# One copy of the queries out of PSUM, and the gated channels turned one step ahead, in a hybrid recurrent, attention and sparse-FFN kernel

## The chip, the cores and the metric

The kernel runs on one core of a Trainium2 chip. The metric is device time in microseconds (us) of one execution; three executions are given and their median counts. TensorE (PE; its weight loads are the row PEld), VectorE (DVE), ScalarE (ACT), GpSimd (POOL) and SyncE (SP, which here only issues DMAs) each work through a queue of their own in order.

## The reference

The input `x` has 4 sequences of 1024 tokens with 256 channels. Four residual layers follow, each on the normalized `x`. The change touches the second and the third:

```python
x = x + lru(layernorm(x))
x = x + ffn(layernorm(x), ...)      # first call: "f1" in the kernel
x = x + attention(layernorm(x))     # 8 heads of 64, full softmax, keys from a latent of 64
x = x + ffn(layernorm(x), ...)      # second call, same weights: "f2"

# attention
q = (x @ Wq.T).reshape(b, t, 8, 64); k, v = up-projections of x @ Wkv_down.T
attn = softmax(q k^T / 8);  out = (attn v).reshape(b, t, 512) @ Wo.T

# ffn: two score vectors per token, each softmax cut to its 32 largest
out_branch = keep32(score_out) * (x @ weight)
in_branch  = (keep32(score_in) * x) @ weight
return out_branch + in_branch + bias
```

`keep32(s)` stands for the softmax with all but its 32 largest values set to zero; the reference writes it with `top_k` and a scatter.

## The kernel before

The work is tiled by 128 tokens: 32 tiles, 8 in a sequence. Stage one (to about 376 us of the profiled execution) holds the recurrent layer, the first eight FFN tiles and the preparation of the attention. Stage two (376 to about 1292 us) is the attention, with 24 FFN tiles of f1 and the heads of f2 interleaved. Stage three is f2's tiles.

Stage two is written as one main generator, `heads`, and a list `side` of generators. `heads` yields 256 times: 4 sequences x 2 halves (`nb`) x 4 pairs of heads (`g`) x 4 query tiles (`q`) x 2 heads (`j`). One such yield is called a step here. Every step makes 128x1024 scores in PSUM (L886, tile `sc`), their negated row maximum (L890, L892, tile `nm`), the exponentials (L894, tile `pr`), and then their transpose: for even `q` ACT and POOL split them into two float16 parts (L897, L898, tile `pd`) and a DMA on SP's queue transposes (L899, tile `d`); for odd `q` PE transposes (L905) and ACT copies (L910, tile `p`). `values_sum` multiplies with the values later (L930, tile `pmo`) and scales (L938, L940, L941).

`merge` takes one step of `heads`, then every side generator whose due time has come; each yield of a side generator moves its due time on by the number, or the next number of the list, given with it. That fixes program order. The order in each engine's queue is then made by the framework's scheduler, which simulates the program with costs of its own, takes program order as priority, and hands out buffers as they come free.

All side work and `pmo` share one PSUM tag, `"s"`, with two buffers: query products `pmq`, FFN logits `pl`, turned channels `px`, FFN products `pf`, output products `pmy`, `pt`, `pc`, `pml`, `pv`. A third tile waits until one of two is released by its last reader.

`queries` is called 32 times, 7 steps before its result is first used. It makes 128x512 query values for a pair of heads in `pmq` (6 matmuls) and needs them in `qs` in two forms: for head j, partitions of that head hold the value rounded to float32r, and the other 64 partitions hold the rest, value minus rounded value. `products` (L170) works in such two-part sums, and `split` (L160, L161) makes the two parts elsewhere, on ACT and DVE.

A fine FFN tile (`tile(..., fine=True)`, 24 of them) yields after its logits and exponentials, three times inside the search for the 32 largest (L674), after the search (L628 to L630), after the out branch (L636; `full` comes from DRAM), and at its end. The in branch scales `x` (L656, L657), gates it (L658, tile `xg`), turns it by two transposes (L682, `px`), splits it (`vt0`, `vt1`), and multiplies (L685 bias, L170 products, `pf`); L662 adds to `x`. With the list `[1, 1, 1, 1, 1, 2, 1]` the in branch runs two steps after the out branch.

Of the kernel before, what the change touches and what calls it, by code (L numbers as in the profile page):

```python
# [10 lines left out]
F32 = mybir.dt.float32  # L11
I32 = mybir.dt.int32
F32R = mybir.dt.float32r
# [3 lines left out]
ALU = mybir.AluOpType  # L17
# [4 lines left out]
P = 128  # L22
# [3 lines left out]
KD = D // P  # L26
# [131 lines left out]
def split(nc, hi, lo, src):  # L158

    last = nc.scalar.copy(hi, src).ins  # L160
    nc.vector.tensor_tensor(lo, src, hi.bitcast(F32), ALU.subtract)  # L161
    return last
# [17 lines left out]
class Banks:  # L180
# [5 lines left out]
    def tile(self, shape, tag, name):  # L186
        return self.pool.tile(shape, F32, tag=tag, name=name, bufs=self.bufs[tag])
# [300 lines left out]
class Ffn:  # L488
# [100 lines left out]
    def tile(self, i, sp, psum, tags, out=None, fast=False, parts=None, tt=None, fine=False):  # L589


        nc, w = self.nc, self.w
        pool = nc.vector if fast else nc.gpsimd
        x = self.x[i]
        blk, tk = i // 4, slice((i % 4) * P, (i % 4 + 1) * P)
        full = None
        if blk in self.full:
            full = sp.tile([P, D], F32, tag="full", name="full")
            nc.sync.dma_start(full, self.full[blk][:, i % 4, :])
        pl = psum.tile([P, 2, D], tags[0], "pl")  # L600
# [12 lines left out]
        nc.gpsimd.tensor_scalar(nm, m8[:, :, 0, 0], -1.0, 0.0, ALU.mult, ALU.add)  # L613
        for s in range(2):
            nc.scalar.activation(  # L615
                ex[:, s, :], pl[:, s, :], AF.Exp, bias=nm[:, s : s + 1], accum_out=ssum[:, s : s + 1]
            )
            self.last_exp = nc.scalar.activation(e8[:, s, :], m8[:, s, 0, :], AF.Exp, bias=nm[:, s : s + 1]).ins
        yield
        for r in range(nr):  # L620
            for s in range(2 if r else 0):
                self.ordered(nc.vector.max, m8[:, s, r, :], wk[:, s, :])
            for s in range(2):
                v, k = (wk, m8[:, s, r, :]) if r else (ex, e8[:, s, :])
                self.ordered(nc.vector.match_replace, wk[:, s, :], k, v[:, s, :], 0.0)
            if fine and r < nr - 1:
                yield
        pool.tensor_tensor(ex, ex, wk, ALU.subtract)  # L628
        rs = sp.tile([P, 2], F32, tag="rs", name="rs")
        nc.vector.reciprocal(rs, ssum)  # L630
        yield

        q = i % 4
        norm = self.norm[blk]
        if full is not None:
            nc.vector.scalar_tensor_tensor(full, full, rs[:, 0:1], ex[:, 0, :], ALU.mult, ALU.mult)  # L636
            ob = full
        else:
            if tt is not None:
                pf = psum.tile([P, D], tags[2], "pf")  # L640
                self.full_product(pf, tt, q)
            else:
                xn = sp.tile([P, D], F32, tag="fxn", name="fxn")
                with self.tc.issue_after(self.convolved):
                    nc.scalar.activation(
                        xn, x, AF.Identity, bias=norm[:, 1, q : q + 1], scale=norm[:, 0, q : q + 1]
                    )
                pf = self.product(sp, psum, tags, xn, None, parts)
            ob = sp.tile([P, D], F32, tag="ob", name="ob")
            nc.scalar.mul(ob, pf, rs[:, 0:1])  # L650
            pool.tensor_tensor(ob, ob, ex[:, 0, :], ALU.mult)  # L651
        yield

        xg = sp.tile([P, D], F32, tag="xg", name="xg", bufs=2)
        sc = sp.tile([P, 2], F32, tag="sc", name="sc")
        pool.tensor_scalar(sc, norm[:, :, q], rs[:, 1:2], 0.0, ALU.mult, ALU.add)  # L656
        nc.scalar.activation(xg, x, AF.Identity, bias=sc[:, 1:2], scale=sc[:, 0:1])  # L657
        pool.tensor_tensor(xg, xg, ex[:, 1, :], ALU.mult)  # L658
        nc.gpsimd.tensor_tensor(x, x, ob, ALU.add)
        pi = self.product(sp, psum, tags, xg, w.bias, parts)  # L660
        if out is None or fast:
            nc.vector.tensor_tensor(x, x, pi, ALU.add)  # L662
        else:
            yi = sp.tile([P, D], F32, tag="yi", name="yi")
            nc.scalar.copy(yi, pi)
            nc.gpsimd.tensor_tensor(x, x, yi, ALU.add)
        if out is not None:
            nc.sync.dma_start(out[i // 4][:, i % 4, :], x)
        yield
# [4 lines left out]
            ins = make(*args).ins  # L674
        self.last_topk = ins if self.keep else None

    def product(self, sp, psum, tags, v, bias, parts):

        nc, w = self.nc, self.w
        px = psum.tile([P, KD, P], tags[1], "px")  # L680
        for k in range(KD):
            nc.tensor.transpose(px[:, k, :], v[:, k * P : (k + 1) * P], w.ident)  # L682
        dst = psum.tile([P, D], tags[2], "pf")
        if bias is not None:
            nc.tensor.matmul(dst, w.ones, bias, start=True, stop=False)  # L685
        if parts:
            vt = [sp.tile([P, KD, P], F32R, tag=f"vt{i}", name=f"vt{i}", bufs=1) for i in range(2)]
            split(nc, *vt, px)
            products(
                nc,  # L690
                dst,
                [([t[:, k, :] for t in vt], [t[:, k, :] for t in parts]) for k in range(KD)],
                start=bias is None,
            )
            return dst
        vt = sp.tile([P, KD, P], F32, tag="vt", name="vt", bufs=2)
        nc.scalar.copy(vt, px)  # L697
        for k in range(KD):
            nc.tensor.matmul(  # L699
                dst, vt[:, k, :], w.wf[:, k, :], start=(k == 0 and bias is None), stop=(k == KD - 1)  # L700
            )
        return dst
# [70 lines left out]
class Attention:  # L773
# [68 lines left out]
    def queries(self, b, nb, g, psum, tag):  # L842

        nc, xnt = self.nc, self.xnt[b, nb]
        qs = self.qs[b, nb, g] = self.wp.tile([P, 2, 512], F32R, tag="qs", name="qs", bufs=2)
        pm = psum.tile([P, 512], tag, "pmq")
        products(
            nc, pm, [([t[:, k, g * P : (g + 1) * P] for t in self.wqk], [t[:, k, :] for t in xnt]) for k in range(KD)]
        )
        for j in range(2):  # L850
            mine, other = slice(j * HD, (j + 1) * HD), slice((1 - j) * HD, (2 - j) * HD)
            nc.scalar.copy(qs[mine, j, :], pm[mine, :])
            nc.vector.tensor_tensor(qs[other, j, :], pm[mine, :], qs[mine, j, :].bitcast(F32), ALU.subtract)  # L853
        yield

    def heads(self, b, psum):
# [183 lines left out]
def tile_kernel(ctx: ExitStack, tc: tile.TileContext, x_in, w_lru, vecs_in, rows, w_ffn, lin_t, w_attn, w_down, out):  # L1040
    nc = tc.nc
# [20 lines left out]
    w = Weights()  # L1062
# [8 lines left out]
    f1 = Ffn("f1", tc, bp, x, w)  # L1071
# [3 lines left out]
    with ExitStack() as c1:  # L1075
        psum = Banks(c1.enter_context(tc.tile_pool(name="ps1", space=PSUM)), {"pu": 2, "po": 2, "py": 2, "pt": 2})
# [38 lines left out]
        k = NBLK - 1  # L1115
# [14 lines left out]
    with ExitStack() as c2:  # L1130
        sp = c2.enter_context(tc.tile_pool(name="at_s", bufs=2))
# [3 lines left out]
        wfs = two([P, KD, D], "wf")  # L1135
# [48 lines left out]
        psum = Banks(c2.enter_context(tc.tile_pool(name="ps2", space=PSUM)), {"sc": 2, "t": 2, "s": 2})  # L1184
        at.hp = c2.enter_context(tc.tile_pool(name="at_h", bufs=1))
        fp = c2.enter_context(tc.tile_pool(name="f_s", bufs=2))
        side = []
# [22 lines left out]
        for i in range(TPB, NT):  # L1210
            n = i - TPB
            start = 1 + 6.75 * n if n < TPB else STEPS * (n // TPB) - STEPS + 48.25 + 8 * (n % TPB + 1)
            side.append((start, f1.tile(i, fp, psum, "sss", parts=wfs, fine=True), [1, 1, 1, 1, 1, 2, 1]))
        merge(chain(*(at.heads(b, psum) for b in range(B))), side)
        for j in range(2):
            last = at.output(B - 1, 1, psum, range(2 * j, 2 * j + 2), slice(PAIRS - 1, PAIRS), True)
# [1 line left out]
    with ExitStack() as c3:  # L1218
        psum = Banks(c3.enter_context(tc.tile_pool(name="ps3", space=PSUM)), {"pl": 2, "px": 3, "pf": 3})
        fp = c3.enter_context(tc.tile_pool(name="f_e", bufs=4))  # L1220
# [104 lines left out]
```

## Time and profile before

| | before |
|---|---|
| median of 3 executions | 1530.5 us (1527.78 to 1530.98) |
| profiled execution, own time | 1528.76 us |
| its span, first to last instruction | 1527.0 us |
| mean granted TensorE clock | 0.946 |
| busy over the span: PE / DVE / ACT / POOL | 84% / 78% / 67% / 45% |

The profile's rows name source line, engine, operation and tiles (`out<-in`), with a count, busy time and the mean duration of one. A row of waits says whose engine stood idle before which instruction, which instruction ended the idle time, then total us, number of times and the longest. A row of the timeline begins with the start and the duration in us; a bracket gives the idle time before the instruction and what ended it.

### The profile page before, as it was taken

The numbers are of one execution on the slowest core, as the hardware profiler recorded it, in microseconds if no ns is written. First come the engines' busy times: TensorE is split into PE (matmuls) and PEld (weight loads), VectorE is DVE, ScalarE is ACT, GpSimd is POOL, SyncE is SP. The second block draws the span as 40 slices with busy tenths as digits, with TensorE's granted clock in tenths as the row PEclk, the third lists the DMA queues.
The fourth block names the chain that finished last, engine by engine and source line by source line (L and its number), as shares of the span: only waits on it lengthen the run. The fifth ranks groups of instructions, "written<-read, shape, count | busy, mean of one in ns | idle before, by whom it ended". The sixth has DMA issues, their size and how long they took to land. (4 is left out here: it accounts for less than half of the span.)

```text
span 1527.0 us, 28727 instructions
## 1 busy us (share of the span) xinstructions
PE 1286.5 (84%) x10134; PEld 955.6 (63%) x10136; DVE 1184.6 (78%) x3682; ACT 1017.5 (67%) x2152; POOL 680.3 (45%) x849
## 2 busy tenths in 40 slices
PE   4879998697898898888998989889999999566675
PEld 3535465376677766766776767677777777334454
DVE  8976665697868887878768687777676675599998
ACT  5353433566887877797777787877777776475674
POOL 2033332161545454544544554454344444067776
PEclk9999999698999999999999999999999999688899
DMA  3110000321454343434433445334344545000000
GB/s 118 32 41 15 21 21 21 128 97 49 84 93 90 61 77 73 77 70 82 82 74 60 72 79 86 61 61 83 68 82 79 92 86 96 1 15 24 22 25 28
DMA packets 288609, 96.51 MB, mean 63 GB/s; under 512 B 268233, under 2 KB 284626, under 8 KB 288466
## 3 DMA queue, kind: packets, MB, share of 16 engines
q1 hardware_dynamic: 283024, 88.50, 28.7%
q10 hardware_dynamic: 5442, 6.18, 1.2%
q8 instruction: 80, 1.31, 0.4%
q14 instruction: 63, 0.52, 0.1%
HBM read 16.01 MB, written 11.53 MB: 18 GB/s over the span
## 5 line engine op out<-in xcount | busy, mean ns | idle before, releaser
L898 POOL TENSOR_TENSOR pd<-pr,pd 128x1024 f16<-128x1024 f32 x128 | 273.5, 2141 | 247.6 <-ACT pd L897 185.7
L890 DVE TENSOR_REDUCE nm<-sc 128x1 f32<-128x1024 f32 x256 | 308.5, 1217 | 78.9 <-PE sc L886 77.5
L894 ACT ACTIVATE pr<-sc,nm 128x1024 f32<-128x1024 f32 x256 | 285.9, 1119 | 84.6 <-DVE nm L892 47.0
L886 PE MATMUL sc<-kh,qs 128*128 128x512 f32 x512 | 184.3, 438 | 26.4 <-ACT pr L894 18.8
L886 PE MATMUL sc<-kl,qs 128*128 128x512 f32 x512 | 162.0, 397 | 0.0
L674 DVE MATCH_REPLACE8 wk<-m,wk 128x256 f32<-128x256 f32 x384 | 154.9, 406 | 0.1
L910 ACT COPY p<-ptp 128x512 f32<-128x512 f32 x224 | 124.1, 590 | 45.3 <-PE ptp L905 33.7
L674 DVE MAX8 m<-wk 128x8 f32<-128x256 f32 x384 | 151.3, 412 | 0.4
L930 PE MATMUL pmo<-p,la 128*64 128x128 f32 x2048 | 144.0, 289 | 6.1 <-ACT ft L524 2.9
L905 PE MATMUL ptp<-ident,pr 128*128 128x128 f32 x1024 | 138.3, 275 | 12.9 <-ACT pr L894 12.4
L930 PEld LDWEIGHTS pmo<-p,la 128*64 128x64 f32 x2048 | 122.8, 144 | 25.0 <-ACT ft L524 5.1
L905 PEld LDWEIGHTS ptp<-ident,pr 128*128 128x128 f32 x1024 | 115.6, 140 | 34.8 <-ACT pr L894 22.2
L897 ACT CAST pd<-pr 128x1024 f16<-128x1024 f32 x128 | 133.5, 1054 | 5.6 <-DMA d<-pd 4.6
L886 PEld LDWEIGHTS sc<-kh,qs 128*128 128x128 f32 x512 | 85.2, 195 | 51.1 <-ACT pr L894 29.8
L886 PEld LDWEIGHTS sc<-kl,qs 128*128 128x128 f32 x512 | 97.0, 190 | 23.2 <-issue 1.4
L930 PE MATMUL pmo<-d,lb 128*64 128x128 f16 x3072 | 103.4, 222 | 7.6 <-DVE qs L853 2.6
L930 PEld LDWEIGHTS <-lb 128*64 128x64 f16 x3072 | 92.2, 111 | 26.3 <-issue 20.1
L628 POOL TENSOR_TENSOR ex<-ex,wk 128x512 f32<-128x512 f32 x61 | 77.6, 1273 | 57.4 <-DVE wk L674 45.5
L926 POOL COPY rows<-rs 128x128 f32<-128x128 f32 x128 | 36.1, 294 | 124.4 <-PE pmo L938 76.3
L941 DVE TENSOR_TENSOR on<-pmo,rb 128x128 f32<-128x128 f32 x128 | 36.4, 285 | 66.8 <-ACT rb L940 66.3
L147 PE MATMUL pt<-ident,xn 128*128 128x128 f32 x256 | 47.8, 309 | 44.5 <-ACT xn L145 32.9
L699 PE MATMUL pf<-wf,vt 128*128 128x256 f32 x288 | 81.2, 427 | 4.6 <-ACT vt L697 4.2
(307 smaller groups left out, 2768.6 us busy)
## 6 DMA issues: line engine op xcount, KB each, us to landing
tt<-ft SPq DMA_DIRECT2D x16, 256.0 KB
tt<-tt SPq DMA_DIRECT2D x8, 512.0 KB
out<-x SPq DMA_DIRECT2D x32, 128.0 KB
x<-in_x ACTq DMA_DIRECT2D x6, 512.0 KB
pf<-pfs SPq DMA_DIRECT2D x12, 256.0 KB
full<-pf SPq DMA_DIRECT2D x24, 128.0 KB
d<-pd SPq DMA_TRANSPOSE x128
wa<-in_w_attn SPq DMA_DIRECT2D x2, 640.0 KB
```

Of the source, the lines that this page charges most:

```text
L147: nc.tensor.transpose(pt[:, k, i * P : (i + 1) * P], xn[:, k * P : (k + 1) * P], ident)
L628: pool.tensor_tensor(ex, ex, wk, ALU.subtract)
L674: ins = make(*args).ins
L699: nc.tensor.matmul(dst, vt[:, k, :], w.wf[:, k, :], start=(k == 0 and bias is None), stop=(k == KD - 1))
L886: nc.tensor.matmul(sc[:, sl], qs[:, j, q * P : (q + 1) * P], kk[:, sl], start=(i == 0), stop=(i == 1))
L890: nc.vector.tensor_reduce(nm, sc, AX.X, ALU.max, negate=True)
L894: nc.scalar.activation(pr, sc, AF.Exp, bias=nm, accum_out=ssum[:, j : j + 1])
L897: nc.scalar.copy(pd[:, 0, :], pr)
L898: nc.gpsimd.tensor_tensor(pd[:, 1, :], pr, pd[:, 0, :], ALU.subtract)
L905: nc.tensor.transpose(pt[:, kk, :], pr[:, kc * P : (kc + 1) * P], self.ident)
L910: nc.scalar.copy(dst, pt)
L930: nc.tensor.matmul(po[j * HD : (j + 1) * HD, 0, :], v, pts[j][:, c, :], start=(n == 0), stop=(n == len(terms) - 1),)
```

## The change

Part one, in `queries`: ACT copies the whole 128x512 product out of PSUM once, into a new float32 tile `q` in SBUF (one buffer). VectorE then copies each head's 64 partitions from `q` to `qs` in float32r, and POOL computes the rest from `q` and `qs`. Before, ACT made each rounded half from PSUM and VectorE each rest from PSUM.

Part two, in `tile` and `product`: a new function `turn` does the two transposes and the split. A fine tile calls it in the in branch's step, yields, and calls `product` with the finished `vt` in the next one. The list of due times changes from `[1, 1, 1, 1, 1, 2, 1]` to eight ones: scaling, gating, the addition of the out branch and turning come one step earlier than before, the product stays at its step. Other callers get `turn` inside `product` in the same order as before.

```diff
@@ tile
-        pi = self.product(sp, psum, tags, xg, w.bias, parts)
+        vt = None
+        if fine:
+            vt = self.turn(sp, psum, tags, xg)
+            yield
+        pi = self.product(sp, psum, tags, xg, w.bias, parts, vt)
@@ Ffn
+    def turn(self, sp, psum, tags, v, parts=True):
+        px = psum.tile([P, KD, P], tags[1], "px")
+        for k in range(KD):
+            self.nc.tensor.transpose(px[:, k, :], v[:, k * P : (k + 1) * P], self.w.ident)
+        if not parts:
+            return px
+        vt = [sp.tile([P, KD, P], F32R, tag=f"vt{i}", name=f"vt{i}", bufs=1) for i in range(2)]
+        split(self.nc, *vt, px)
+        return vt
+
+    def product(self, sp, psum, tags, v, bias, parts, vt=None):
+        nc, w = self.nc, self.w
+        if vt is None:
+            px = self.turn(sp, psum, tags, v, False)
         dst = psum.tile([P, D], tags[2], "pf")
         if bias is not None:
             nc.tensor.matmul(dst, w.ones, bias, start=True, stop=False)
         if parts:
-            vt = [sp.tile([P, KD, P], F32R, tag=f"vt{i}", name=f"vt{i}", bufs=1) for i in range(2)]
-            split(nc, *vt, px)
+            if vt is None:
+                vt = [sp.tile([P, KD, P], F32R, tag=f"vt{i}", name=f"vt{i}", bufs=1) for i in range(2)]
+                split(nc, *vt, px)
@@ queries
+        q = self.wp.tile([P, 512], F32, tag="q", name="q")
+        nc.scalar.copy(q, pm)
         for j in range(2):
             mine, other = slice(j * HD, (j + 1) * HD), slice((1 - j) * HD, (2 - j) * HD)
-            nc.scalar.copy(qs[mine, j, :], pm[mine, :])
-            nc.vector.tensor_tensor(qs[other, j, :], pm[mine, :], qs[mine, j, :].bitcast(F32), ALU.subtract)
+            nc.vector.tensor_copy(qs[mine, j, :], q[mine, :])
+            nc.gpsimd.tensor_tensor(qs[other, j, :], q[mine, :], qs[mine, j, :].bitcast(F32), ALU.subtract)
@@ tile_kernel
-            side.append((start, f1.tile(i, fp, psum, "sss", parts=wfs, fine=True), [1, 1, 1, 1, 1, 2, 1]))
+            side.append((start, f1.tile(i, fp, psum, "sss", parts=wfs, fine=True), [1, 1, 1, 1, 1, 1, 1, 1]))
```

More of the change, by code (lines that the diff above doesn't have):

```diff
@@ L675, in ordered @@
         self.last_topk = ins if self.keep else None
-    def product(self, sp, psum, tags, v, bias, parts):
-        nc, w = self.nc, self.w
+    def turn(self, sp, psum, tags, v, parts=True):
         px = psum.tile([P, KD, P], tags[1], "px")
         for k in range(KD):
-            nc.tensor.transpose(px[:, k, :], v[:, k * P : (k + 1) * P], w.ident)
+            self.nc.tensor.transpose(px[:, k, :], v[:, k * P : (k + 1) * P], self.w.ident)
[8 more added lines that the diff above has]
+            px = self.turn(sp, psum, tags, v, False)
         dst = psum.tile([P, D], tags[2], "pf")
```

## The prediction

> **What bounds the kernel now.** I first cut the span where the change lies, from the first score product to the last (busy time by window: PE, PEld, DVE, ACT, POOL; the counts in brackets).
>
> ```profile
> 376.00:1292.00 916.00, 822.39 (x8245) 655.14 (x8246) 687.13 (x1714) 700.90 (x1366) 428.76 (x420) 0.98 0.42 77
> ```
>
> PE works 822 of 916 us, 90%; ACT 77%, DVE 75%, POOL 47%. A step is 916/256 = 3.6 us. Nothing but PE can set this stage for long, so a gain must come out of PE's idle 93.6 us. Outside this stage no queue changes except for one query group at 365 us, which is used 8 us after it is done. Next I read what ended PE's idle time there.
>
> ```profile
> PE sc L886 <- ACT pr L894: 18.8, 22, 2.8
> PE ptp L905 <- ACT pr L894: 12.4, 16, 1.8
> PE pt L147 <- DVE qs L853: 9.0, 5, 2.1
> PE sc L886 <- DVE qs L853: 6.7, 7, 1.7
> PE pf L170 <- DVE nm L892: 5.1, 6, 1.3
> PE pmo L930 <- DVE qs L853: 4.4, 5, 1.6
> ...
> PE pf L170 <- ACT vt L160: 3.7, 9, 0.7
> ...
> PE pf L170 <- DVE vt L161: 3.0, 4, 1.5
> ...
> PE pmy L170 <- DVE qs L853: 2.6, 2, 1.3
> ```
>
> Four rows end with L853, the old query subtraction. Three of them (`pt`, `pmo`, `pmy`: 16.0 us) have no use for queries: they wait for a PSUM buffer of tag "s" that `pmq` holds. The fourth (`sc`, 6.7 us, 7 times) waits for the queries. Three rows (`pf`: 11.8 us) are the FFN product waiting for its split. The change aims at these 34.5 us. Then the timeline of one late query group, and rows on the port that POOL and DVE share:
>
> ```profile
> 804.29 1.62 PE L170 MATMUL pmq<-xnt,wqk 128*128 128x512 f32 x6
> 808.38 0.58 ACT L852 CAST qs<-pmq 64x512 fp32r<-64x512 f32 x1
> 810.49 2.14 POOL L898 TENSOR_TENSOR pd<-pr,pd 128x1024 f16<-128x1024 f32 x1 [2.50 <-ACT pd L897]
> 810.58 0.68 DVE L853 TENSOR_TENSOR qs<-pmq,qs 64x512 fp32r<-64x512 f32 x1
> 811.32 0.72 PE L886 MATMUL sc<-kh,qs 128*128 128x512 f32 x2 [1.66 <-DVE qs L853]
> 811.81 0.58 ACT L852 CAST qs<-pmq 64x512 fp32r<-64x512 f32 x1
> 813.99 0.69 DVE L853 TENSOR_TENSOR qs<-pmq,qs 64x512 fp32r<-64x512 f32 x1
> ```
>
> ```profile
> L636 DVE SCALAR_TENSOR_TENSOR full<-full,rs,ex x24: 474/864/2319, 402.1 to 1063.7; 128x256 f32<-128x256 f32 x24
> L853 DVE TENSOR_TENSOR qs<-pmq,qs x64: 683/689/694, 367.3 to 1255.3; 64x512 fp32r<-64x512 f32 x64
> L953 POOL TENSOR_TENSOR onp<-on,onp 128x512 fp32r<-128x512 f32 x28 | 35.9, 1280 | 20.3 <-ACT onp L952 16.3 <-DVE m L674 3.1 <-PE ptp L905 0.9
> L269 DVE TENSOR_SCALAR t<-st,cs_s 128x256 f32<-128x256 f32 x1 | 0.3, 339 | 0.0
> L269 DVE TENSOR_SCALAR t<-st,cs_s 128x128 f32<-128x128 f32 x1 | 0.3, 272 | 0.0
> ```
>
> In the timeline the PSUM buffer is held from 804.29 to 814.68, 10.4 us, because four instructions of two queues read it in turn, each late in its queue. Read off the same way, the 32 groups hold it 7.8 us on average, and 3.0 us up to the end of ACT's first copy.
>
> **The change part by part.**
>
> *Part one, PSUM.* ACT's single copy has the shape of L910's (590 ns). The buffer is free at its end: 3.0 us instead of 7.8. Of the 16.0 us of buffer waits I take away three quarters, **-12 us**; the rest stays because the copy itself can be late, as above (pmq done at 805.91, copy at 808.38). If the freed buffer is at once taken by other late work, it is worth nothing.
>
> *Part one, ACT.* 64 copies of 580 ns go, 37.1 us; 32 of 590 come, 18.9. ACT loses 18.2 of its 701 us. PE waits 31.2 us for `pr`; in proportion that is 0.8: **-1 us**.
>
> *Part one, POOL.* 64 subtractions of 64x512 come. The nearest row is L953, same output type and 512 elements, 1280 ns: +82 us, POOL to 56%. Half the partitions may make it no cheaper; less than 0.7 us (L658's 256 elements) or more than twice L953 has no row behind it. They write other partitions than they read, which no POOL row of before does. POOL itself is covered by its idle 487 us. Queued behind them are L898 and L926. Each subtraction first waits for VectorE's copy, so a `pd` can be late by that wait and 1.3 to 2.6 us, and its transposing DMA on SP with it; the rows of PE's waits have 1.9 us in all for these DMAs, so I cost it at 0, and at 32 x 1 us if the cover is gone.
>
> *Part one, VectorE.* 64 subtractions of 689 ns go: -44.1 us. 64 copies SBUF to SBUF come. No such copy is in the trace; L269 (one SBUF source) grows by 67 ns for 128 elements, so 512 cost 339 + 2 x 67 = 473 ns, 30.3 us. At the rate of a PSUM source it would be 690. Here a rule speaks against the change. L636 (two SBUF inputs) took 474 ns alone, up to 2319, 972 on average, while L853 with one PSUM input never left 683 to 694. The Trainium skill, "SBUF — State Buffer", "Who interferes with whom", says that VectorE and POOL share a port pair as an exclusive lock, that a VectorE copy in a two-port mode needs it, and that the loser waits for the whole instruction of the other. By the L853 row alone the new copies are free of it: -14 us of VectorE time. By the rule they wait like L636, 0.50 us each (which agrees with a 47% busy POOL and half of a 2.14 us `pd`): +32, so +18 net. A second copy right behind the first may find the port still its own, +16, so +2. I take the rule and the middle, +10, and +2 for L636-like rows under a fuller POOL (24 x 0.5 x 82/429). That is 1.7% of VectorE's time; a quarter of it on PE's path is **+3 us**.
>
> *Part one, lateness.* Now the first half is ready when one subtraction ends, 1.4 us after ACT's first copy (mean of 32). Afterwards: the same queue wait on VectorE (0.7), lock 0.5, copy 0.47, POOL's queue 0.3, subtraction 1.28: 3.2 us, **1.8 us later**; if a `pd` stands ahead in POOL's order, up to 5. In 25 groups the queries are ready 6 us or more before use, and it costs nothing. In the 7 rows above it is on PE's path: 7 x 1.8 = 13 us, up to 35. But those groups are late since their product had to wait for a buffer, which now comes earlier. I take half of 13: **+7 us**.
>
> *Part two.* POOL's `sc`, ACT's `xg`, POOL's gating and `x` addition, two transposes, ACT's and VectorE's split: all exist before and only come one step earlier; no DMA is issued in that step (`full` is loaded at the tile's start, on SP). POOL stands at L656 for VectorE's `rs` already (45.2 us of its waits), with `pd` behind it; one step earlier can lengthen that, at POOL's cost alone. What moves on PE: the product no longer waits for a split issued just before, 11.8 us. A step of 3.6 us covers ACT's 0.39 and VectorE's 0.41 with their queues. Against it, the transposes follow the gating more closely (0.4 us of waits now); I let 3 us remain: **-9 us**. If the scheduler puts product right behind turn again, 0. Bias product and `pf` no longer take the second PSUM buffer while `px` holds the first; the row for that is small and I count nothing.
>
> Sum: -12 - 1 + 3 + 7 - 9 = -12 us. A PE at 90% hands some of it back in new waits for `pr`; I take **-10**. On the profiled execution's own 1528.76 us (span 1527.0 plus 1.8 around it) that gives 1518.8. The median is 1.7 higher, so I forecast 1530.5 - 10 = **1520.5 us**.
>
> **The rivals.**
>
> *Late queries (slower).* The score product waits for POOL. For: POOL's order is strict, `pd` takes 2.14 us, the copy in front can be locked out as long, and the late groups are the rule in the second and third sequence (slack 0.1 us). Price: if the buffers do not bring their products forward and a `pd` lies ahead, 7 x 5 = +35, and part one's other terms -12 - 1 + 3; with part two at 0 to -9 the end is 1530.5 + 16 to + 25, 1547 to 1556; with a delay of 3.5 us (+25) and half the buffer gain, 1530.5 + 25 - 7 + 3 - 9 = 1543. It decides from about 3.5 us of delay on the seven groups (25 us), where it outweighs the 22 us of -12, -1 and -9 with the +3. Against: POOL is half idle and the other 25 groups have slack.
>
> *Stalls re-form (no change).* The buffer waits turn into waits for `pr`, as ACT and VectorE are at three quarters and the scores have two buffers only. For: the two largest rows are these. Then 1528 to 1533.
>
> *The order does not follow.* The engines' order comes from a simulated schedule. If product follows turn at once, and freed buffers go to lower-priority work, the edit does less than it says: -1 + 3 + 13 = +15, 1545.
>
> *More than forecast.* All 16.0 and 11.8 us go and the late groups (6.7) vanish, less 3: -31, 1499.
>
> **How the numbers follow.** As forecast, 1508 to 1527: 0.44. More than that: 0.06. Within 0.2% of 1530.5 (1527.4 to 1533.6; about what a measurement of this kernel can tell from no change): 0.12. Late queries: 0.28, order: 0.10. So faster 0.50, same 0.12, slower 0.38. Faster and slower both hold much; the likeliest case alone is 1508 to 1527. For 8 in 10 the range goes from 1504 to 1546, leaving about one in ten out at either end.
>
> **What would show it.** Right: the rows `pt`, `pmo`, `pmy` <- qs nearly gone, `pf` rows below 4 us in sum, VectorE's copies near 0.5 us with a maximum near 2.5 (lock), POOL's subtractions at 1.28 us. Wrong: `sc` <- POOL `qs` over 20 us, or PE's idle time in this stage still above 90 us with `pr` as releaser. A PE busy time that differs by more than 5 us would mean that something outside these waits moved.

## The result: slower by 0.4%, where faster by 10 us was forecast

| | before | after |
|---|---|---|
| median | 1527.93 us (22 executions) | 1534.76 us (22 executions) |
| ratio, 95% interval | | 1.004 [1.003, 1.005] |
| profiled execution, own time | 1528.76 us | 1535.12 us |
| its span | 1527.0 us | 1533.4 us |
| mean granted TensorE clock | 0.946 | 0.931 |
| PE busy over the span | 1286.5 us | 1300.0 us |

The change costs 6.8 us by the medians and 6.4 us by the two profiled executions. PE executes the same matmuls in both (10134 and 10136 of them are in the traces) and is busy 13.5 us longer. The profile after, busy time by window (columns: length, then PE, PEld, DVE, ACT, POOL with counts, granted clock, DMA share, GB/s), cut late in stage one, at the first score product and at the end of the last:

```profile
0.00:291.40 291.40, 239.22 (x884) 144.71 (x884) 217.17 (x791) 124.76 (x239) 79.14 (x159) 0.93 0.15 51
291.40:380.90 89.50, 72.71 (x320) 53.19 (x319) 74.14 (x304) 53.02 (x128) 37.95 (x54) 0.84 0.19 65
380.90:1298.90 918.00, 828.57 (x8248) 659.66 (x8249) 692.57 (x1715) 681.41 (x1336) 513.31 (x483) 0.97 0.43 77
1298.90:1533.40 234.50, 159.50 (x688) 105.78 (x686) 208.40 (x874) 136.39 (x418) 136.81 (x218) 0.82 0.06 20
```

The same view of before:

```profile
0.00:290.00 290.00, 237.09 (x884) 144.08 (x884) 216.73 (x791) 124.64 (x239) 78.29 (x157) 0.94 0.12 39
290.00:376.00 86.00, 69.83 (x319) 51.99 (x318) 71.87 (x304) 53.59 (x129) 36.03 (x54) 0.88 0.31 109
376.00:1292.40 916.40, 822.79 (x8248) 655.44 (x8249) 687.37 (x1714) 701.30 (x1367) 429.11 (x421) 0.98 0.42 77
1292.40:1527.00 234.60, 156.83 (x688) 104.10 (x686) 208.63 (x874) 137.99 (x418) 136.89 (x218) 0.85 0.07 21
```

Read length minus PE busy as PE's idle time. Stage one: 4.9 us longer, all of it busy time (306.9 to 311.9). Stage two: 1.6 us longer, made of 5.8 us more busy time and 4.2 us less idle time (93.6 to 89.4). Stage three: unchanged in length. So PE's idle time in stage two did shrink, by less than half of the forecast, and two things outweigh that gain: stage two starts late, and PE takes longer for the same matmuls while the granted clock is lower in every row.

What ended PE's idle time in stage two of after (who waits, what released it; total us, times, longest; the rows used below, the others are left out):

```profile
PE sc L903 <- ACT pr L911: 23.1, 25, 2.7
PE ptp L922 <- ACT pr L911: 16.2, 20, 1.9
PE pmq L170 <- DVE on L958: 9.1, 5, 2.2
PE pmo L947 <- DVE on L958: 4.6, 6, 2.0
PE pf L170 <- DVE nm L909: 3.7, 5, 1.1
PE pmo L947 <- ACT q L866: 2.8, 4, 0.9
PE pmo L947 <- DMA d<-pd: 2.7, 3, 1.8
PE pf L170 <- ACT vt L160: 2.2, 6, 0.4
PE sc L903 <- POOL qs L870: 2.2, 3, 0.9
PE pl L554 <- DVE on L958: 1.4, 1, 1.4
PE px L685 <- DVE on L958: 0.8, 2, 0.4
PE pf L170 <- DVE vt L161: 0.6, 1, 0.6
PE pmy L170 <- DVE on L958: 0.6, 1, 0.6
```

The rows of before that end with the scaling of the attention's result (`on`):

```profile
PE pmy L170 <- DVE on L941: 1.5, 1, 1.5
PE pt L147 <- DVE on L941: 1.3, 1, 1.3
PE pmo L930 <- DVE on L941: 0.6, 1, 0.6
PE pf L685 <- DVE on L941: 0.5, 2, 0.3
```

The three rows `pt`, `pmo`, `pmy` behind the query subtraction (16.0 us before) are gone; 2.8 us behind the new copy `q` are what is left of them. The score product's wait for queries fell from 6.7 us to 2.2. In their place stand waits for the same two PSUM buffers, now released by `on`: 16.5 us in five rows (9.1 + 4.6 + 1.4 + 0.8 + 0.6), where `on` ended 3.9 us before. The waits for `pr` grew from 31.2 to 39.3 us.

The queries themselves (minimum, median, maximum in ns), two rows of VectorE by shape (busy us and mean ns), and one slow copy in the timelines of POOL and VectorE (its row holds a pair of copies; the first ends at 471.09):

```profile
L869 DVE CAST qs<-q x64: 397/424/2255, 370.6 to 1258.2; 64x512 fp32r<-64x512 f32 x64
L870 POOL TENSOR_TENSOR qs<-q,qs x64: 1259/1295/1469, 371.8 to 1259.8; 64x512 fp32r<-64x512 f32 x64
```

```profile
L869 DVE CAST qs<-q 64x512 fp32r<-64x512 f32 x64 | 33.4, 522 | 9.1 <-ACT q L866 8.1
L636 DVE SCALAR_TENSOR_TENSOR full<-full,rs,ex 128x256 f32<-128x256 f32 x24 | 29.6, 1232 | 11.3 <-POOL ex L628 11.3
```

```profile
468.66 2.15 POOL L915 TENSOR_TENSOR pd<-pr,pd 128x1024 f16<-128x1024 f32 x1 [3.29 <-issue]
469.86 1.68 DVE L869 CAST qs<-q 64x512 fp32r<-64x512 f32 x2
```

POOL's subtraction costs what its nearest row said. Of VectorE's 64 copies, 58 took 397 to 426 ns. The other six took 1226 to 2255 ns; each began while a `pd` subtraction was running on POOL, and each ended about 0.28 us after that subtraction did.

**Where stage two loses its start.** Before 360 us the change itself adds no instruction to any queue, and yet the queues differ. SyncE's timeline, first of before, then of after:

```profile
263.14 28.28 SPq L527 DMA_DIRECT2D tt<-ft  x6
293.53 0.83 SPq L561 DMA_DIRECT2D tt<-tt  x2
294.41 1.50 SPq L712 DMA_DIRECT2D wa<-in_w_attn  x2
```

```profile
264.52 0.51 SPq L527 DMA_DIRECT2D tt<-ft  x1
267.28 0.82 SPq L561 DMA_DIRECT2D tt<-tt  x2
268.15 0.91 SPq L727 DMA_DIRECT2D wa<-in_w_attn  x2
...
280.86 11.88 SPq L527 DMA_DIRECT2D tt<-ft  x4
```

The attention's weights (`wa`) are loaded 26 us earlier, in front of four of the recurrent layer's transfers. PE's queue is ordered differently too, and this is what it does some 30 us ahead of the attention, first before, then after:

```profile
349.34 1.99 PE L567 MATMUL pfa<-wf,tt 128*128 128x256 f32 x8 [2.04 <-ACT ob L650]
352.78 1.13 PE L567 MATMUL pf<-wf,tt 128*128 128x256 f32 x4 [1.45 <-ACT pfs L581]
```

```profile
348.18 0.38 PE L685 MATMUL px<-ident,xg 128*128 128x128 f32 x2
354.36 2.07 PE L567 MATMUL pf<-wf,tt 128*128 128x256 f32 x4 [5.81 <-ACT pfs L581]
```

Before, the eight `pfa` products stand between two short waits. After, they come later and PE stands still for 5.81 us in one piece; then the four `pf` products take 2.07 us instead of 1.13. The trace's clock records explain the second number:

```
granted clock up to 384 us, from the last rise ahead of these products (start, length in us)
before   1.0 from 311.2, 58.0   0.5 from 369.2, 10.2
after    1.0 from 305.3, 47.8   0.5 from 353.0,  6.8   1.0 from 359.9, 13.7   0.5 from 373.5, 10.2
```

Over the span, PE ran at half clock for 164.5 us before and 211.6 us after (54.6 to 68.8 in stage one, 37.5 to 57.5 in stage two, 72.4 to 85.3 in stage three). What that does to one matmul is seen in stage two of after: the score product of `kh` takes 630 ns in the median for the 20 that lie wholly in a stretch of half clock, and 396 ns for the 490 outside.

### The profile page after: what moved, and what is told of

Same layout as the page of the kernel before. It is cut to its first block, busy times and chain, and to the rows that moved or that the text cites. A ratio compares the mean times of both kernels' runs of the same rounds, so it can differ in the third digit from the quotient of the medians.

```text
span 1533.4 us, 28814 instructions
## 1 busy us (share of the span) xinstructions
PE 1300.0 (85%) x10136; PEld 963.3 (63%) x10136; DVE 1192.3 (78%) x3682; ACT 995.6 (65%) x2120; POOL 767.2 (50%) x913
## 4 chain that ended last, share of the span: by engine, by line
PE 43%; DVE 33%; ACT 11%; issue 5%; POOL 4%; DMA 2%; ACTq 0%; POOLq 0%; DVEq 0%
PE sc L903 9%; PE pmo L947 8%; DVE wk L678 7%; DVE nm L907 6%; DVE m L678 5%; PE ptp L922 4%; ACT pr L911 3%; PE po L437 3%; PE pmy L170 2%; PE pu L170 2%; POOL qs L870 2%; PE pl L556 2%; PE pz L452 1%; PE pfa L567 1%; ACT pd L914 1%
## 5 line engine op out<-in xcount | busy, mean ns | idle before, releaser
L903 PE MATMUL sc<-kh,qs 128*128 128x512 f32 x512 | 189.3, 447 | 26.5 <-ACT pr L911 23.1
L922 PE MATMUL ptp<-ident,pr 128*128 128x128 f32 x1024 | 139.5, 278 | 16.5 <-ACT pr L911 16.2
L947 PE MATMUL pmo<-p,la 128*64 128x128 f32 x2048 | 138.9, 281 | 5.3 <-ACT ft L524 1.5
L947 PEld LDWEIGHTS pmo<-p,la 128*64 128x64 f32 x2048 | 117.0, 139 | 26.0 <-issue 5.3
L870 POOL TENSOR_TENSOR qs<-q,qs 64x512 fp32r<-64x512 f32 x64 | 86.5, 1352 | 67.9 <-DVE qs L869 65.2
L714 PE MATMUL pf<-wf,vt 128*128 128x256 f32 x288 | 85.3, 439 | 3.3 <-ACT vt L712 2.6
```

The lines of the kernel that those rows point to most:

```text
L714: nc.tensor.matmul(dst, vt[:, k, :], w.wf[:, k, :], start=(k == 0 and bias is None), stop=(k == KD - 1))
L870: nc.gpsimd.tensor_tensor(qs[other, j, :], q[mine, :], qs[mine, j, :].bitcast(F32), ALU.subtract)
L903: nc.tensor.matmul(sc[:, sl], qs[:, j, q * P : (q + 1) * P], kk[:, sl], start=(i == 0), stop=(i == 1))
L922: nc.tensor.transpose(pt[:, kk, :], pr[:, kc * P : (kc + 1) * P], self.ident)
L947: nc.tensor.matmul(po[j * HD : (j + 1) * HD, 0, :], v, pts[j][:, c, :], start=(n == 0), stop=(n == len(terms) - 1),)
```

## The experiments

All are compared with before, which was measured again beside each group of kernels (medians of 1527.9 to 1530.2 us); a ratio, with its 95% interval, is against that before. "Start" is the first score product in the profiled execution: 376.0 us before, 380.9 after. Where an engine's order of instructions is said to be that of another kernel, it was read from the two traces.

### Part two alone

```diff
 (the change, but queries as before: two copies by ACT, two subtractions by VectorE from PSUM)
```

> Part two alone: fine tiles turn and split one step ahead, queries as before. If part two does its own work and part one carries the loss, this is 5 to 9 us faster than before (1519 to 1523) with the waits of the FFN product (11.8 us) cut to 4 to 7. If the loss lies in part two, it is about as slow as the changed kernel (1533 to 1536). If any change of the program moves the time by what a new instruction order brings, it lands anywhere within 8 us of before, whatever its waits do.

Measured: 1540.22 us, 1.0071 [1.0055, 1.0086]. Part two alone is no gain but the larger loss. The profiled execution puts it into the first sequence of stage two, 231.4 us long against 220.3:

```profile
378.50:609.90 231.40, 203.50 (x1925) 160.43 (x1925) 185.50 (x473) 177.57 (x357) 112.39 (x116) 0.96 0.45 78
```

PE has 44 more matmuls there than before (1881), is busy 8.0 us longer and idle 3.1 us longer. The separate step has moved work into this sequence, and the next two give only 2.7 us back. The start is 2.5 us later than before although no engine's order differs from before ahead of 400 us, so a shift of this size is what single executions differ by.

### Part one alone

```diff
 (before, with the change's queries: one copy, q, VectorE copies, POOL subtracts)
```

> Part one alone: one copy out of PSUM, split by VectorE and POOL; FFN tiles as before. If VectorE and POOL locking each other out carries the loss (late row maxima), this is as slow as the changed kernel or slower (1534 to 1542), with VectorE's copies at 0.5 us and more and the exponentials' waits for nm above 85 us. If part one is sound, it is 3 to 8 us faster than before. If the order alone decides, it is anywhere within 8 us, and the stage before the attention is some 4 us longer than before, as in the changed kernel.

Measured: 1532.43 us, 1.0015 [1.0001, 1.0029]. Start at 380.8, as late as with the whole change; the second sequence is 8.6 us shorter than before. A late start and a gain in stage two stand side by side, so part one has to be taken apart.

### The buffer alone

```diff
+        if (b, nb, g) == (0, 0, 0):
+            q = self.wp.tile([P, 512], F32, tag="q", name="q")
+            nc.gpsimd.memset(q[:, 0:1], 0.0)
         for j in range(2):   # queries as before
```

> The kernel before with the new tile q reserved in SBUF but used by nothing (one element column is cleared once by POOL). No engine has other work. If the new buffer alone changes where tiles lie and with it the order of all queues, the first score product comes 2 to 5 us later as in the changed kernel and the time differs from before by 2 to 8 us. If the loss comes from the work that the change moves, this equals before within 0.2%.

Measured: 1533.74 us, 1.0028 [1.0019, 1.0038]. The place is reserved and hardly touched, and the kernel is slower by more than with part one whole. Windows and the same stop in PE's timeline of this kernel:

```profile
291.00:379.50 88.50, 72.69 (x319) 53.18 (x318) 73.00 (x303) 53.62 (x129) 35.47 (x53) 0.85 0.20 66
379.50:1299.90 920.40, 827.30 (x8248) 660.68 (x8249) 687.66 (x1714) 700.41 (x1367) 428.79 (x421) 0.97 0.43 77
```

```profile
353.84 2.07 PE L567 MATMUL pf<-wf,tt 128*128 128x256 f32 x4 [5.81 <-ACT pfs L581]
```

The same 5.81 us of standing still, the same 2.07 us, half clock from 352.7 for 6.8 us, `wa` loaded at 267.60. In stage two its idle time is that of before (93.1 us) and its busy time is 4.5 us more, with 48.2 us of half clock. So both halves of the loss, the late start and the slower matmuls, appear with the reserved place alone. The profiled execution is the slowest of its 14 (1537.38 us), so the size of the second half is overstated here.

The early order follows the full place without exception. Five kernels reserve it in this pool (after, and the experiments of this section, the one before and the next, and "Subtraction on VectorE"): all load `wa` at 267.6 to 269.5 us, all have the stop of 5.81 us, and they start at 379.5 to 381.5. The other twelve, before among them, load `wa` at 293.7 to 297.0, stop for at most 2.04 us there and start at 374.3 to 378.7. Up to the first query group at 370 us every engine's order in this kernel is that of after. By which path a place in SBUF changes the schedule no run shows.

### First query group in the old form

```diff
+        if tag == "at":  # the group made ahead of stage two
+            (old copies and subtractions)
+        else:
             (the change's)
```

> The changed kernel, but the one query group that is made before the attention stage is made in the old way. If the 4.9 us that the changed kernel loses before its first score product come from that group's longer chain (copy, copy, subtraction on three engines), the first score product returns to about 376 us and the total falls by 3 to 5 us. If they come from the buffer and the order, the first score product stays at 380 us and the total at 1533 to 1537.

Measured: 1534.37 us, 1.0025 [1.0011, 1.0039]. Start still at 381.5. The chain of copy, copy and subtraction of the first group is not what delays stage two.

### The buffer in a pool that is opened later

```diff
-        q = self.wp.tile([P, 512], F32, tag="q", name="q")
+        q = self.hp.tile([P, 512], F32, tag="q", name="q")   # part one alone, first group in the old form
```

> Part one alone, with the new tile q placed in the pool of the attention stage that is opened last, and the first query group made in the old way, so that nothing before the attention stage has reason to move. If the buffer in the early pool costs 3 to 5 us before the first score product, that product is back at 376 to 377 us and the time falls to 1524 to 1528, below before, with the granted clock near 0.944. If part one has no gain of its own, the time stays at 1530 to 1534.

Measured: 1534.73 us, 1.0029 [1.0018, 1.0040], start at 378.7. Ahead of the attention this gives the old order back (`wa` at 296.71 us, no stop of 5.81 us), and the start lies at the upper end of the kernels with that order. The expected gain did not come: stage two takes 921.7 us, against 912.9 in part one alone. With the new place in another pool the loss lies in stage two.

### Subtraction on VectorE

```diff
-            nc.gpsimd.tensor_tensor(qs[other, j, :], q[mine, :], qs[mine, j, :].bitcast(F32), ALU.subtract)
+            nc.vector.tensor_tensor(qs[other, j, :], q[mine, :], qs[mine, j, :].bitcast(F32), ALU.subtract)
```

(in part one alone)

> Part one alone, but the subtraction is VectorE's too, from q and qs in SBUF; POOL gets no new work. If POOL's 82 us of subtractions and the port that it shares with VectorE carry a loss in part one, this is 2 to 6 us faster than part one with POOL (1532.4), with the exponentials' waits for nm lower. If VectorE's own time matters more (64 subtractions of about 0.7 us and 64 copies), it is 2 to 6 us slower. If neither, it is within 2 us.

Measured: 1563.56 us, 1.0214 [1.0201, 1.0228], 31 us more than part one alone. The stage's window, and VectorE's subtraction by shape:

```profile
381.50:1328.90 947.40, 832.40 (x8248) 663.85 (x8249) 727.49 (x1776) 682.69 (x1336) 436.13 (x421) 0.97 0.42 75
```

```profile
L855 DVE TENSOR_TENSOR qs<-q,qs 64x512 fp32r<-64x512 f32 x64 | 56.3, 880 | 2.0
```

A loss of 2 to 6 us was the case nearest to this. VectorE is busy 727 us of 947, PE's idle time rises to 115 us, and the stage is 34.5 us longer than in part one alone (912.9 us). The exponentials wait for VectorE's row maxima 126.6 us, against 92.3 in part one alone: 34.3 us more. So a subtraction of 56.3 us on VectorE delays the row maxima, though it is busy only 77% of the stage; a share that the new order has in this was not separated. In part one alone POOL takes the same 64 subtractions, is busy 56% of the stage, and PE waits 1.7 us for them. Giving the subtraction to POOL is the sound part of the change.

### Turned at the old due times

```diff
-                [1, 1, 1, 1, 1, 1, 1, 1]
+                [1, 1, 1, 1, 1, 2, 0, 1]      # part two alone: a yield, but turn and product in one step
```

> Part two alone with the due times of before: scaling, gating and turning stay two steps after the out branch and the product follows in the same step; only the order of split and bias product differs in program order. If the loss of part two (10.9 us) comes from moving the gating and turning a step forward, this equals before within 3 us. If it comes from the new order that any change of these instructions brings, it is 4 to 12 us slower than before.

Measured: 1529.54 us, 1.0000 [0.9990, 1.0011]. Start 374.4, first sequence 220.9 us. Every engine executes its instructions in the order of before, from beginning to end, so this is before once more: the rewritten functions and the added yield change nothing, and the loss of part two alone comes with its due times. Whether asking for the gating earlier does it, or any new order would, this run cannot tell, as it made no new order.

### A buffer of half the size

```diff
-            q = self.wp.tile([P, 512], F32, tag="q", name="q")
+            q = self.wp.tile([P, 256], F32, tag="q", name="q")   # the reserved place again
```

> The kernel before with a reserved tile of half the size of q (256 columns), one column cleared once by POOL. The order before the attention stage stays as before almost to its end. If the loss of the reserved full tile (4.4 us) comes from the stage before the attention (first score product at 379.5 us), this has its first score product at 376 us and loses at most 2 us. If the attention stage's own new order counts, it differs from before by 2 to 6 us in either direction.

Measured: 1528.93 us, 0.9992 [0.9983, 1.0001]. Start 376.0.

```profile
290.00:376.00 86.00, 70.87 (x319) 52.62 (x319) 71.69 (x303) 53.35 (x129) 36.20 (x55) 0.88 0.32 109
376.00:1289.70 913.70, 818.50 (x8248) 651.58 (x8249) 687.12 (x1714) 701.59 (x1367) 429.43 (x421) 0.99 0.43 78
```

The extra instruction on POOL is the same as with the full buffer, and the loss is gone. It is the size of the reserved place that sets off the other order. But for that one column this kernel does the very work of before, and every engine does it in the order of before, from beginning to end. So the 4.3 us by which its PE busy time in stage two differs from before, with 26.8 us of half clock instead of 37.5, is what two executions of one order differ by.

### Part one without a new buffer

```diff
-        q = self.wp.tile([P, 512], F32, tag="q", name="q")
+        q = self.sp.tile([P, KD, 256], F32, tag="ft", name="q", bufs=1).rearrange("p a b -> p (a b)")
```

`q` shares the buffer of the FFN's tile `ft`.

> Part one alone without a new buffer: q takes the SBUF tile ft of the same size, which only the heads of f2 use 14 times. The order before the attention stage stays as before almost to its end. If part one gains 3 to 4 us inside the attention stage and loses 4 to 5 before it only through the buffer, this is 3 to 6 us faster than before (1524 to 1527) with the clock at 0.943 or more. If part one has no gain of its own, 1528 to 1534.

Measured: 1525.54 us, 0.9975 [0.9963, 0.9987]. Part one is a gain once nothing is reserved for it: 0.40% between this and part one alone.

### Product one step later

```diff
-                [1, 1, 1, 1, 1, 1, 1, 1]
+                [1, 1, 1, 1, 1, 2, 1, 1]      # part two alone: turn at the old step, product one later
```

In this kernel the last tile of a sequence is added after the next sequence's normalization has read it: that addition is left out of what the attention sees, and a wait with it.

> Part two alone, but scaling, gating and turning stay at the step of before and the product goes one step later. The split still lies one step ahead of its product, so the waits of the FFN product fall as with part two. If the loss of part two (10.9 us) comes from the gating chain being asked for a step earlier, this is within 3 us of before. If any spacing of the two steps gives it (a new order, less often a full clock), it is 4 to 12 us slower.

Measured: 1536.44 us, 1.0044 [1.0027, 1.0061]. This is the second case: another spacing of the two steps costs time too, without any earlier gating, though this kernel has the omission in it. Moving the product instead of the turning is no remedy.

### Both parts, no new buffer, at three due times

The old step for turn and product (`[1, 1, 1, 1, 1, 2, 0, 1]`):

> Part one without a new buffer, and part two with the due times of before (turning and product in one step). If the two losses found (the buffer and the earlier step) are all that stands against the change, this is the fastest kernel: 1523 to 1527. If every rewrite draws a new order whose idle stretches and clock scatter by a few us, it lies between 1525 and 1536 and the clock tells where.

Measured: 1527.47 us, 0.9981 [0.9970, 0.9992]. Every engine's order is that of part one without a new buffer (1525.54 us), so this says nothing of part two; the 1.9 us between the two medians, of 22 executions each, are what one order measured twice differs by.

The product one step later (`[1, 1, 1, 1, 1, 2, 1, 1]`, with the omission of the kernel above):

> Part one without a new buffer, and part two with the product one step later instead of the gating one step earlier. If only the earlier gating harms, 1522 to 1528. If the split ahead of its product harms in itself, it is slower than before by 3 to 10 us, as part two alone.

Measured: 1506.72 us, 0.9853 [0.9829, 0.9877]. It would be the fastest, but for what it leaves out. The same with the last tile of each sequence begun half a step earlier, so that nothing is left out:

```diff
+            start -= 0.5 if n % TPB == TPB - 1 else 0
```

> Part one without a new buffer; turning at its old step and the product one step later, with the last tile of each sequence half a step earlier so that its sum is read by the next sequence as in the reference. If the gain of e12 (22 us) came from the wait that it left out, this is back at 1522 to 1532. If it came from the later product, it is at 1505 to 1512.

Measured: 1526.54 us, 0.9979 [0.9969, 0.9989]. So the 22 us hung on the omission, and the later product is worth nothing by itself. That they are a wait at the sequences' boundaries is not shown: the same omission in part two alone brought nothing (1536.44 us with it, 1533.69 without, below).

### The whole change without its buffer

```diff
-        q = self.wp.tile([P, 512], F32, tag="q", name="q")
+        q = self.sp.tile([P, KD, 256], F32, tag="ft", name="q", bufs=1).rearrange("p a b -> p (a b)")
```

> The whole change, but q takes the tile ft and no new buffer is reserved. If the buffer is the larger part of the loss, this is at 1526 to 1530, at or below before. If part two with its earlier step is the larger part, it stays at 1533 to 1540.

Measured: 1523.94 us, 0.9962 [0.9948, 0.9975], faster than before by 6.2 us and than the change as made by 10.8 us. Its windows and a part of PE's timeline (this profiled execution took 1528.17 us, near the top of its twelve):

```profile
290.00:376.60 86.60, 71.10 (x325) 52.56 (x323) 71.70 (x304) 53.45 (x129) 38.64 (x56) 0.87 0.32 111
376.60:1292.80 916.20, 824.88 (x8248) 658.28 (x8249) 689.74 (x1714) 682.63 (x1336) 513.99 (x483) 0.97 0.42 77
```

```profile
349.98 1.99 PE L567 MATMUL pfa<-wf,tt 128*128 128x256 f32 x8 [2.04 <-ACT ob L650]
353.42 1.13 PE L567 MATMUL pf<-wf,tt 128*128 128x256 f32 x4 [1.45 <-ACT pfs L581]
```

The old order is back ahead of stage two: short waits around `pfa`, products of 1.13 us, start at 376.6, `wa` loaded at 295.24. Profile against profile, the start is 4.3 us of the 6.9 us between this kernel and after, and 3.6 of the 5.5 us between part one with and without the new place.

### Part two alone, product late, nothing left out

```diff
-                [1, 1, 1, 1, 1, 1, 1, 1]
+                [1, 1, 1, 1, 1, 2, 1, 1]
+            start -= 0.5 if n % TPB == TPB - 1 else 0
```

> Part two alone with turning at its old step and the product one step later, the last tile of each sequence half a step earlier. If the earlier gating is what harms in part two, this is within 3 us of before. If every spacing of the two steps harms, 1534 to 1542 as e1 and e10, with a clock near 0.932.

Measured: 1533.69 us, 1.0016 [0.9998, 1.0034]: not told from no change, and 3.5 us above before by the medians, just outside either case. So whether the earlier gating or the spacing of the two steps harms in part two stays open.

### The clock beside the busy time

Stage two of six profiled executions, all with the same 8248 matmuls (one execution each; the buffer alone was the slowest of its 14, the small buffer among the fastest of its 14):

| | PE busy | PE idle | half clock |
|---|---|---|---|
| small buffer | 818.5 | 95.2 | 26.8 |
| part one, no buffer | 818.3 | 93.3 | 27.3 |
| before | 822.8 | 93.6 | 37.5 |
| change, no buffer | 824.9 | 91.3 | 48.1 |
| buffer alone | 827.3 | 93.1 | 48.2 |
| after | 828.6 | 89.4 | 57.5 |

Busy time follows the half-clock time, about a third of a microsecond for each (10.1 us more busy time for 30.7 us more at half clock from the first to the last row), and idle time does not. Over all 17 profiled kernels, which have the same 8248 matmuls there, it is 0.29 us for each (correlation 0.87; of idle time with half clock 0.25). Median clocks over all executions agree in direction: 0.944 before, 0.933 after, 0.9435 for the change without its buffer. Within the 22 executions of after, one program in one order, the time runs from 1538.5 us at a clock of 0.928 to 1527.0 at 0.940, on a fitted line by 9.1 us for each 0.01 (correlation -0.89). By that line, an estimate, the 0.011 between the medians of before and after go with 10 us, more than the 6.8 us of the result. But a longer stop both costs time and lowers the clock, and no run held the clock fixed while the order changed. That the lower clock makes the matmuls longer is seen; how much of the difference in time it causes, beyond the busy time above, stays open.

## Why the prediction was wrong

**The step that failed** is the sentence "Outside this stage no queue changes except for one query group at 365 us", and with it that the new tile `q` was costed at nothing. The prediction knew that the order comes from a simulated schedule in which buffers are handed out as they come free, and used that only for the product's place. But with the place of a new 512-column float32 tile the order of all queues was another from 267 us on, 100 us ahead of the first query group, also where the tile was hardly used. The place alone costs 0.28% (buffer alone), 0.40% within part one, and 0.78% within the whole change (1.004 against 0.9962; 10.8 us between the medians). Half the place leaves the order as it was and costs nothing. For kernels without the new place the sentence holds: up to the first query group every engine keeps the order of before. In the profiled executions the 16.4 us between the forecast of -10 and the measured +6.4 are 4.9 of stage one and 5.8 of busy time in stage two (both fixed in the prediction), 5.8 of idle time that was expected to go and stayed, and -0.1 of stage three. The 5.8 of busy time are not all the buffer's: two executions of one order differed by 4.3. The prediction's last test, PE busy time differing by more than 5 us, was met: 13.5.

**The rest of the forecast** has the right sign and is too large. Without the buffer the change gains 6.2 us (4 to 8 by its interval); that is another kernel than the one forecast, and most of its gain is part one's.

- *PSUM, -12.* Right in its own terms, not in its worth. By the same reading of the timelines as before, the 32 groups hold the buffer 3.4 us (7.8 before; forecast 3.0), and of the 16.0 us of waits 2.8 are left, behind the new copy `q`: 13.2 less. But 12.6 us came back as waits behind `on` (16.5 less the 3.9 of before): the freed buffer is taken at once by other work, the case that the prediction named and did not choose. The hand back of 2 us was the second term that failed, by its size: the rows that the change aims at lost 23.0 of their 34.5 us, and PE's idle time only 4.2, so 18.8 us were handed back.
- *ACT, -1.* ACT lost 19.9 us of busy time in stage two (forecast 18.2); the `pr` waits grew all the same, from 31.2 to 39.3 us, so they do not follow ACT's load.
- *POOL.* 64 subtractions at 1352 ns in the mean (forecast 1280), +84 us of POOL. Its cover held: `pmo` waits for the transposing DMA were 2.7 us (1.9 before).
- *VectorE, +3.* The rule of the port lock held and the row of L853 did not: 397/424/2255 ns, and the slow copies end with POOL's instruction. The free copy is cheaper than estimated (424, not 473) and the lock costs it 0.1 us in the mean, not 0.5. The lock fell on others: L636 rose from 972 to 1232 ns in the mean, 6.2 us where 2 were forecast. The sum in stage two is +5.2 us, not +12.
- *Lateness, +7.* Too high. The score products waited 2.2 us in 3 cases. The first half was ready 2.9 us after ACT's copy on average (3.2 worked out, 1.4 before), the second 4.3 (4.8 before). But only 3 groups were still used as soon as they were ready, where before it was 7.
- *Part two, -9.* The waits for `vt` and its neighbours on `pf` L170 fell from 11.8 us to 6.5, where below 4 was named, and were worth almost nothing: the whole change without the buffer (0.9962) and part one without it (0.9975) have overlapping intervals. Alone it costs 0.71%, and only with its new due times (at the old ones the order is that of before). Why it costs so much alone, above all in the first sequence, and nothing beside part one is not settled.

**The rivals.** Late queries, which would have given the right sign, is refuted by 2.2 us against the 25 from which it decides. "The order does not follow" came nearest: the order did move against the change, but by the buffer and ahead of stage two, not by where the product stands. "Stalls re-form" describes stage two of the profile well, but `on` took over the larger part, not `pr`.

## What to carry to other kernels

Where a scheduler hands out buffers and makes the queues' order, a new tile is a change to everything: price it by reserving the place alone, at two sizes, before judging the edit that needs it, and look for an existing buffer that can lend its place. Read PE's idle and busy time apart, by stage, with the granted clock beside them: the same matmuls that take longer are no wait, and no row of waits will show them. And when a wait for one of two buffers is taken away, ask who stands next in line for them; here 16.0 us left three rows, and 15.4 stand behind `on` and `q` in their place. When two kernels differ by a few us, compare the order of their instructions first: two of the experiments above, meant to test a rewrite, had made no new order at all.

## What the runs showed of the hardware that was not expected

The half clock does not need a long stop. At 348.56 us of after PE stood still for 5.81 us and half clock began at 353.0, which agrees with the Trainium skill, "TensorE: Matmul & The Clock Gate", "Part 1: The HAM clock gate (the "warmup" mystery)": the clock falls after at least one idle window of about 3.4 us. In stage two, however, PE's longest stop was 2.77 us before and 2.69 us after, and still the clock fell there 8 times before and 12 times after, 3.4 or 6.8 us each time. So the measurement decides.

The stretches of the clock records are multiples of 3.41 us. Cut stage two of all 17 profiled kernels into windows of this length, laid as the records lie, and take those at full clock. The clock fell after each of the 87 windows in which PE stood still for 2.0 us or more in sum, after 40 of 52 with 1.8 to 2.0 us, after 42 of 656 with 0.8 to 1.8, and after none of 3543 with less. A stop of 2.10 us in before (from 904.47 us) is cut in two by the border of a window, and the clock stays; one of 2.21 us in after (from 955.08) lies in one window, and the clock falls. The windows, first of before, then of after (length, then busy time of PE, PEld, DVE, ACT, POOL; the granted clock is the third number from the end):

```profile
901.68:905.10 3.42, 2.35 (x9) 1.35 (x8) 3.42 (x11) 3.37 (x8) 0.29 (x1) 1.00 0.00 0
905.10:908.51 3.41, 1.94 (x14) 1.71 (x15) 3.35 (x9) 3.41 (x7) 3.31 (x2) 1.00 0.02 5
```

```profile
953.79:957.20 3.41, 1.30 (x6) 0.73 (x4) 3.27 (x7) 0.00 (x0) 2.64 (x2) 1.00 0.54 102
957.20:960.62 3.42, 3.16 (x7) 2.05 (x8) 3.11 (x7) 1.48 (x3) 0.19 (x1) 0.50 1.10 205
```

This fits that less idle time went with more half clock: after has 12 stops of 1.8 us or more in stage two and before 7, and ten windows with that much idle time against five.

POOL's subtraction of 64 partitions into the other 64 takes 1295 ns, no more than 128 partitions in place (1280) and no less. And the port that VectorE and POOL share holds up a small instruction as long as a large one: of VectorE's 21 additions of 128x4 at L65 (`ax_t`), six took 1.0 to 2.1 us in after, and each ended within 0.03 us of an instruction that was running on POOL; two took over 0.6 us before. The mean rose from 226 to 640 ns. That is no rule for all of them: L66 (`norm_f`), of the same shape, fell from 329 to 230 ns. How many are hit differs from one order to another.
